# A tuned convolution block on Trainium2: one order of instructions on all engines, and the sampling's source blocks by DMA from a copy transposed once

## The chip, the cores and the metric

The kernel runs on one core of one Trainium2 chip. The core has five engines that run their own instruction streams side by side and wait for each other by semaphores: TensorE (PE, matrix products, with its weight loads listed as PEld), VectorE (DVE), ScalarE (ACT), GpSimd (POOL) and SyncE (SP, which here only issues DMAs). TensorE writes into PSUM, which is allocated in eight banks of 128 x 512 float32 values; the others mostly work in SBUF. The metric is the device time of one execution in microseconds. All data are float32.

## The reference

The input x has 32 images of 96 channels, 56 x 56 pixels. Two layers follow each other. The first is an inverted bottleneck: a 1x1 convolution to 576 channels, a 3x3 depthwise convolution, a squeeze-and-excite gate, a 1x1 convolution back to 96, and the input added. The second gates its input by a channel gate and a pixel gate (both computed from the image's spectrum), and convolves the gated image twice, once plainly and once with deformed sampling points:

```python
# first layer (bn: a per-channel scale and shift; fq: 8-bit rounding of the weights)
h = silu(bn1(conv1x1(x, fq(w1))))                    # 96 -> 576
h = silu(bn2(depthwise3x3(h, fq(w2))))
h = h * sigmoid(se_w2 @ silu(se_w1 @ mean(h) + se_b1) + se_b2)
x = x + bn3(conv1x1(h, fq(w3)))                      # 576 -> 96
# second layer
mag = abs(rfft2(x));      ca = channel_gate(mag)     # 96 values per image
sa = pixel_gate(mean_c(x), l2_c(x), resize(mean_c(mag)))   # 56 x 56 values
y = x * ca * sa
freq = resize(mean_c(abs(rfft2(y))))
aux = concat(y, coord, freq)
offset = conv3x3(aux, off_w)                         # 9 taps x (dx, dy) for each pixel
gate = sigmoid(conv1x1(relu(conv3x3(aux, dg1_w)), dg2_w))
y_base = conv3x3(y, base_w)
sampled = bilinear(y, pixel + offset)                # 9 samples per pixel and channel
y_def = einsum(sampled, def_w)
z = (1 - gate) * y_base + gate * y_def
out = relu(batchnorm(z) + x)                         # mean and variance over all 32 images
```

## The kernel before, in words

Work is laid out channels on partitions, pixels along the row. Images follow each other in a software pipeline; in the time of one image b the kernel samples and convolves b, computes the gates of b+1 and the hidden layer of b+2.

**The band loop** (`layers`, the loop over `bands`). An image is cut into 7 bands of 8 rows, and a band into two halves of 7 tiles (a tile is 4 columns wide and a half covers 28 columns; each tile has two 4-row groups). A half runs so:

- The bilinear sampling is a matrix product. For each tile the 8 x 8 pixels around it (64 source pixels, `NS`) are the contraction: `yt` holds these source blocks with pixels on partitions and channels along the row, 128 partitions for the two row groups; `wc` holds, for each source pixel, the sampling weight towards each tap of each output pixel. `sample_tiles` (L721) multiplies the two and ScalarE copies the result out of PSUM into `v` (L725). `pack` (L732) moves the last two taps beside the others, and `deform` (L740) applies `def_w` one half later.
- `yt` comes from `block_channels`: GpSimd copies the 8 x 8 blocks, with channels on partitions, from the padded gated image `yp` into `ybl` (L703, two copies for a half, one buffer), TensorE transposes seven blocks for each half into two banks (L707), ScalarE copies them into `yt` (L709).
- `wc` comes from `weights_load` and `weights`: four DMAs on SP spread the column weights and the row weights of a half over 128 partitions (`wc` L685, `wr` L686), and VectorE multiplies them (L692). `prepare` issues the loads, at the start of a half.
- After each tile of a half the loop calls `next(more)` and `pump()`. `more` is the generator `offsets` for the band two ahead: the joint 3x3 convolution of gate, offset and a third of the base (L605), the rest of the base convolution (L633), the offsets to DRAM (`od`, L655) and back (`ht`, L667), two ScalarE steps (L670, L671), and the finished hat functions to DRAM (`hd`, L674).

**The pump.** `pump` advances two generators: `first(b+2)` is `hidden`, whose depthwise taps are VectorE's multiply-adds (L261), with its expansion on TensorE (L168, evicted at L172) and its store `h2d` (L223); `second(b+1)` is `attend`: the projection from `h2d` (`hq` L305, L323, L329), the residual sum on GpSimd (L466), the spectrum (`dft_mag`: x loads L361, products L386 and L410, squares L413, sums L414, root L417), the gates, the spectrum of the gated image (L366 gates it on GpSimd), and the results `ca`, `sa`, `fq`. There are 17 pump steps in a band, 119 in an image. Each generator has a due time for its next step, a linear share of the image:

```python
streams[:] = [[second(b + 1), 0, n_second, slot + 3, slot + length - 8],
              [first(b + 2), 0, n_first, slot, slot + length]]
```

From band 5 (`turn`) the next image replaces this one in `yp`: `refill` loads rows of x1 (L584), the pixel gate `sab` (L586), and VectorE multiplies (L592).

**What sets the order of the work.** Every engine runs its own queue in order. Only SP's queue stands in the order of the text; the order on the other four is made by the framework's scheduler, which rearranges their instructions by its own costs:

```python
with tc.manual_schedule(engines={mybir.EngineType.SP}):
    layers(tc, a, dp, x1d, zd, stats, far)
```

PSUM is split into six banks that rotate (`mm`), one for the gates (`acc`) and one for the deformed convolution (`pd`). After the last image `normalise` reads z and x1 again, scales and writes the output.

## Time and profile before

| | |
|---|---|
| median of 3 runs | 9654.11 us (9645.51 to 9654.31) |
| profiled execution, its own time | 9648.5 us |
| its span, first to last instruction | 9646.7 us |
| mean granted TensorE clock | 0.923 |
| busy: PE, DVE, ACT, POOL | 8472.7, 7227.2, 5322.1, 2532.6 us |
| DMA | 1485.98 MB, mean 154 GB/s |

The page shows the busy time and share of each engine; the span in 40 slices, one digit each, busy share in tenths; the granted clock of TensorE in the same slices; then groups of instructions by line: destination and source, shapes, count, busy time, mean nanoseconds of one, the idle time of the engine just before them and what ended it. A row of waits names the waiting engine and line, what it waited for, the total in us, the number of times, and the longest. A row of windows gives, for a stretch, the busy time of PE, PEld, DVE, ACT and POOL (with the number of instructions), the granted clock, the share of the 16 DMA engines and the GB/s moved. The last 2.5% of the span are `normalise`, with the DMA engines full at 417 GB/s.

### The profile page before, as it was taken

To read this page: it belongs to the slowest core of one execution; us is meant where nothing else is said; L and a number is where in the kernel's file an instruction comes from. 1 tells how busy PE (TensorE), PEld (TensorE's weight loads), DVE (VectorE), ACT (ScalarE), POOL (GpSimd) and SP (SyncE) were. 2 spreads that over 40 slices of the span, in tenths; PEclk is the share of its full clock that TensorE was granted. 3 is DMA by queue.
4 is the path that set the end of the run, shared out by engine and by line. 5 is a ranking of instruction groups with operands and counts; after the bars stand their busy time and mean duration, and the time that the engine had idled before them with its cause. 6 is when DMAs were issued, how large, how long until landed. Compare 5 with 4: busy or idle time off the path is not lost. (4 is left out here: it accounts for less than half of the span.)

```text
span 9646.7 us, 129705 instructions
## 1 busy us (share of the span) xinstructions
PE 8472.7 (88%) x48374; PEld 5064.2 (52%) x48374; DVE 7227.2 (75%) x6948; ACT 5322.1 (55%) x10262; POOL 2532.6 (26%) x2642
## 2 busy tenths in 40 slices
PE   6889989998999999999899989999999999999870
PEld 3455555555555555555555555555555555555540
DVE  7688777778777787877777887777878777777323
ACT  2355555565555556555555655555555555565453
POOL 1123223222222322222232322233222323322210
PEclk9899999999999999999999999999999999999985
DMA  2355555555555555555555555555555555554449
GB/s 94 95 143 148 151 152 160 150 149 143 147 155 154 160 154 145 145 149 155 154 160 155 145 142 153 151 158 154 153 139 145 150 157 157 153 152 135 130 154 417
DMA packets 1069473, 1485.98 MB, mean 154 GB/s; under 512 B 590438, under 2 KB 840086, under 8 KB 1056550
## 3 DMA queue, kind: packets, MB, share of 16 engines
q1 hardware_dynamic: 858747, 985.20, 37.9%
q10 hardware_dynamic: 153803, 329.80, 9.2%
q0 software_dynamic: 56288, 162.60, 6.7%
q8 instruction: 388, 6.36, 0.3%
q14 instruction: 247, 2.02, 0.1%
HBM read 1064.29 MB, written 412.65 MB: 153 GB/s over the span
## 5 line engine op out<-in xcount | busy, mean ns | idle before, releaser
L261 DVE SCALAR_TENSOR_TENSOR acch<-hp,w,acch 128x1512 f32<-128x1512 f32 (+1 forms) x2250 | 4320.5, 1920 | 32.8
L605 PE MATMUL mm<-yp,c_jointW 104*128 104x448 f32 x4032 | 1649.0, 561 | 9.0 <-ACT yt L709 5.5
L740 PE MATMUL pd<-v,c_def 128*96 128x224 f32 (+1 forms) x6272 | 1414.8, 376 | 127.6 <-ACT v L732 104.1
L703 POOL COPY ybl<-yp 96x448 f32<-96x448 f32 x896 | 1014.7, 1159 | 1903.7 <-PE mm L707 1903.3
L721 PE MATMUL mm<-wc,yt 64*96 64x144 f32 x12544 | 1168.1, 308 | 153.5 <-DVE yb L638 76.8
L740 PEld LDWEIGHTS pd<-v,c_def 128*96 128x96 f32 (+1 forms) x6272 | 1051.8, 173 | 437.4 <-ACT v L732 142.5
L168 PE MATMUL mm<-xt,w 96*128 96x392 f32 (+3 forms) x2688 | 1136.3, 561 | 133.8 <-ACT yt L709 96.0
L605 PEld LDWEIGHTS mm<-yp,c_jointW 104*128 104x128 f32 x4032 | 783.6, 196 | 806.0 <-issue 762.6
L721 PEld LDWEIGHTS mm<-wc,yt 64*96 64x96 f32 x12544 | 884.2, 167 | 489.8 <-issue 188.0
L221 ACT ACTIVATE acch<-acch,sh,inv 128x1568 f32<-128x1568 f32 x288 | 487.5, 1693 | 1159.0 <-DVE acch L261 1143.9
L692 DVE TENSOR_TENSOR wc<-wc,wr 128x1008 f32<-128x1008 f32 x448 | 564.6, 1260 | 704.2 <-DMA wr<-hd 690.5
L725 ACT COPY v<-mm 96x288 f32<-96x288 f32 (+1 forms) x2688 | 1003.6, 442 | 117.7 <-PE mm L721 78.9
L172 ACT ACTIVATE hp<-mm,sh,inv 128x392 f32<-128x392 f32 (+2 forms) x1216 | 811.8, 672 | 326.9 <-PE mm L168 282.1
L633 PE MATMUL mm<-yp,c_base0W 96*64 96x448 f32 x4032 | 913.5, 550 | 0.0
L323 PE MATMUL mm<-hq,w3s 128*96 128x392 f32 x2048 | 788.2, 531 | 127.4 <-DMA hq<-h2d 125.9
L655 POOL DMA_DIRECT2D od<-at x224 | 186.3, 832 | 2275.1 <-DVE at L651 1451.9
L732 ACT COPY v<-v 32x448 f32<-32x448 f32 x1344 | 755.3, 562 | 30.3
L168 PEld LDWEIGHTS mm<-xt,w 96*128 96x128 f32 (+1 forms) x2688 | 389.9, 189 | 495.1 <-issue 264.8
L709 ACT COPY yt<-mm 128x384 f32<-128x384 f32 (+1 forms) x896 | 350.9, 441 | 491.5 <-PE mm L707 489.4
L323 PEld LDWEIGHTS mm<-hq,w3s 128*96 128x96 f32 x2048 | 336.3, 173 | 477.7 <-issue 382.5
L466 POOL TENSOR_TENSOR o<-o,xc 96x392 f32<-96x392 f32 x256 | 396.5, 1549 | 643.9 <-ACT o L333 642.3
L633 PEld LDWEIGHTS mm<-yp,c_base0W 96*64 96x64 f32 x4032 | 294.6, 134 | 515.5 <-issue 490.2
(194 smaller groups left out, 9023.7 us busy)
## 6 DMA issues: line engine op xcount, KB each, us to landing
h2d<-acch ACTq DMA_DIRECT2D x288, 784.0 KB
wc<-hd SPq DMA_DIRECT2D x896, 252.0 KB
wr<-hd SPq DMA_DIRECT2D x896, 252.0 KB
hq<-h2d SPq DMA_DIRECT2D x128, 980.0 KB
hq<-h2d SPq DMA_DIRECT2D x128, 784.0 KB
x<-x1d SPq DMA_DIRECT2D x768, 98.0 KB
ht<-od SPq DMA_DIRECT2D x224, 252.0 KB
hd<-ht ACTq DMA_DIRECT2D x224, 252.0 KB
```

What stands on the lines that cost most here:

```text
L168: nc.tensor.matmul(pt[p0 : p0 + w1.shape[1], : rows * W], w1, xts[hf][:, r0 * W : (r0 + rows) * W], start=True, stop=True)
L172: nc.scalar.activation(h1[lo:hi, row0 : row0 + rows, 1 : 1 + W], pt[lo:hi, : rows * W].rearrange("p (h w) -> p h w", h=rows), AF.Silu, bia ...
L261: nc.vector.scalar_tensor_tensor(acc[:, lo:hi], win, wk, acc[:, lo:hi], ALU.mult, ALU.add)
L323: nc.tensor.matmul(pts[half][:C, :EW], w3s[:, ch], hq, start=(i == 0), stop=False)
L605: nc.tensor.matmul(view, weights[:, k], yp[:channels, r0 : r0 + RB, dx + PD - 1 : dx + PD - 1 + W], start=(k == 0), stop=(k == NTAP - 1))
L633: nc.tensor.matmul(pb[k % 2 * BC : (k % 2 + 1) * BC, :BW].rearrange("p (h w) -> p h w", h=RB), w["base"][:, k], yp[:C, r0 : r0 + RB, dx + ...
L692: nc.vector.tensor_tensor(wc, wc, wr, ALU.mult)
L703: nc.gpsimd.tensor_copy(yb[:, :, s], blocks)
L721: nc.tensor.matmul(pt[k][:C, (t - lo) * KP : (t - lo + 1) * KP], yt[ps, t], s[ps, t * KP : (t + 1) * KP], start=True, stop=True)
L725: nc.scalar.copy(v[:C, :, lo:hi, k].rearrange("c k t p -> c t k p"), pt[k][:C, : (hi - lo) * KP].rearrange("c (t k p) -> c t k p", t=hi - ...
L732: nc.scalar.copy(v[C:, 1 + 2 * i : 3 + 2 * i], v[i * QC : (i + 1) * QC, KA:])
L740: nc.tensor.matmul(out.rearrange("c q (t x) -> c t q x", x=TS), p["w"]["def"][ks, k], v[ks, k].rearrange("c t s (r x) -> c t (s r) x", r=T ...
```

## The change

1. `manual_schedule()` names no engine: all five engines take their instructions in the order of the text, without the scheduler.
2. The text is rewritten for that. `attend`, `squeeze`, `dft_mag` and `offsets` are cut into smaller steps, with a `yield` between a product and what reads it; `hidden` yields after every tap, and expands the next image's first unit at the end of this one. `pump` takes exactly one step of `attend` in a slot, from slot 3 on. The two square roots of an image wait (`at_conv`) until the loop comes past a joint convolution.
3. The source blocks come from DRAM. When a row group of the gated image has been written to `yp` and multiplied, TensorE transposes it once (`turn_rows`, four products, one for each column phase), ScalarE copies it out, and GpSimd's queue stores it into `turned`, a copy laid out [column phase, row, column group, channel], one for each of two images. `block_load` reads a half's `yt` with four DMAs on SP. `block_channels` goes, and `yt` has three buffers where it had two. The order of the source pixels in a block is now columns first, so the two broadcasts of `wc` and `wr` are exchanged.
4. `prepare` is called after the weights of a half have been multiplied, for one half further ahead, and loads `yt` along with `wc` and `wr`. The first rows of the next image are asked for in band 4, not 5.

```diff
-        nc.sync.dma_start(wc[ps], src[2 * s].unsqueeze(0).to_broadcast([SB, SB, NTH * KP]))
-        nc.sync.dma_start(wr[ps], src[2 * s + 1].unsqueeze(1).to_broadcast([SB, SB, NTH * KP]))
+        nc.sync.dma_start(wc[ps], src[2 * s].unsqueeze(1).to_broadcast([SB, SB, NTH * KP]))
+        nc.sync.dma_start(wr[ps], src[2 * s + 1].unsqueeze(0).to_broadcast([SB, SB, NTH * KP]))
...
-def block_channels(nc, p, yp, j, h):
+def turn_rows(nc, p, yp, r0, r1):
+    n = (r1 - r0) * NTY
+    every = yp[:C, PD + r0 : PD + r1].rearrange("c h w -> c (h w)").rearrange("c (n x) -> c x n", x=TS)
+    pt = bank(p)
+    for x in range(TS):
+        nc.tensor.transpose(pt[:n, x * C : (x + 1) * C], every[:, x], p["w"]["ident"][:C, :C])
+    return pt
+
+def store_turned(nc, p, pt, yT, r0, r1):
+    n = (r1 - r0) * NTY
+    yq = p["yq"].tile([RB * NTY, TS, C], FP, name="yq")
+    nc.scalar.copy(yq[:n].rearrange("p x c -> p (x c)"), pt[:n, : TS * C])
+    nc.gpsimd.dma_start(yT[:, PD + r0 : PD + r1].rearrange("x h t c -> (h t) x c"), yq[:n])
+
+def block_load(nc, p, yT, j, h):
     yt = p["yt"].tile([2 * NS, NTH, C], FP, name="yt")
-    yb = p["ybl"].tile([C, NTH, 2, SB, SB], FP, name="ybl")
-    src = yp[:C, j * RB : j * RB + SB, h * NTH * TS : h * NTH * TS + SB]
     for s in range(2):
-        blocks = bass.AP(src.tensor, src.offset + s * TS * WY, [src.ap[0], [TS, NTH], [WY, SB], [1, SB]])
-        nc.gpsimd.tensor_copy(yb[:, :, s], blocks)
-    for lo, hi in ((0, 4), (4, NTH)):
-        pt = bank(p)
-        for t in range(lo, hi):
-            nc.tensor.transpose(pt[:, (t - lo) * C : (t - lo + 1) * C], yb[:, t].rearrange("c s r x -> c (s r x)"),
-                                p["w"]["ident"][:C, :C])
-        nc.scalar.copy(yt[:, lo:hi].rearrange("p t c -> p (t c)"), pt[:, : (hi - lo) * C])
+        for g in range(2):
+            r0, t0 = j * RB + s * TS, h * NTH + g
+            q0 = s * NS + g * TS * SB
+            nc.sync.dma_start(yt[q0 : q0 + TS * SB], yT[:, r0 : r0 + SB, t0 : t0 + NTH])
     return yt
...
         def start(b, length):
-            streams[:] = [[second(b + 1), 0, n_second, slot + 3, slot + length - 8],
-                          [first(b + 2), 0, n_first, slot, slot + length]]
+            streams[:] = [[second(b + 1), 0, slot + 3], [first(b + 2), 0, slot, length]]
...
+        def attended(b, args, r, r1):
+            attend_rows(nc, p, b, *args)
+            later.append((slot + 3, lambda: turn(b, r, r1)))
+
+        def turn(b, r, r1):
+            pt = turn_rows(nc, p, yp, r, r1)
+            later.append((slot + 1, lambda: store_turned(nc, p, pt, turned[b % 2], r, r1)))
...
             for h in range(2):
                 v = p["vp"].tile([128, NTAP, NTH, 2, TP], FP, name="v")
-                prepare(2 * n + h + READY + AHEAD)
                 s = ready.pop(0)
                 yt = yts.pop(0)
...
                         ready.extend(weights(nc, *ws) for ws in loads[:1])
                         del loads[:1]
-                        if h == 0:
-                            yts.append(block_channels(nc, p, yp, j, 1))
+                        prepare(2 * n + h + READY + AHEAD + 1)
+                        if b + 1 < B and j == TURN - 1 and h == 1:
+                            refill(b + 1, TURN * RB - PD)
...
-    with tc.manual_schedule(engines={mybir.EngineType.SP}):
+    with tc.manual_schedule():
         layers(tc, a, dp, x1d, zd, stats, far)
```

In `offsets` the distances change like this (the old form had seven steps between the `od` store and the `ht` load, and six from there to L670):

```diff
+    od = p["dp"].tile([NTX, 2, NOFF, TP], FP, name="od")
+    nc.gpsimd.dma_start(od.rearrange("t s o p -> o (t s) p"), at.rearrange("o t s p -> o (t s) p"))
     pb = bank(p)
...
     nc.vector.tensor_tensor(yb[:BC], yb[:BC], pb[BC:, :BW], ALU.add)
-    for _ in range(4):
-        yield
+    yield
+    nc.vector.tensor_reduce(top, at.rearrange("o t s p -> o (t s p)"), AX.X, ALU.max, apply_absolute_value=True)
+    yield from wait(2)
     ht = p["ht"].tile([SB * NTX, 4, KP], FP, name="ht")
...
     nc.sync.dma_start(ht.rearrange("q n k -> q (n k)"), src)
-    for _ in range(6):
-        yield
-    p["tc"].keep_in_program_order(nc.scalar.activation(ht, ht, AF.Abs, bias=w["blk"]))
+    yield from wait(4)
+    nc.scalar.activation(ht, ht, AF.Abs, bias=w["blk"])
```

## The prediction

> **What bounds the kernel now.** I read the page's parts 1 and 2 first, then TensorE's waits, the windows of one image, and last the DMA share of very short windows.
>
> ```profile
> span 9646.7 us, 129705 instructions
> PE 8472.7 (88%) x48374; PEld 5064.2 (52%) x48374; DVE 7227.2 (75%) x6948; ACT 5322.1 (55%) x10262; POOL 2532.6 (26%) x2642
> PE   6889989998999999999899989999999999999870
> PEclk9899999999999999999999999999999999999985
> 600.00:8880.00 8280.00, 7597.75 (x43811) 4542.08 (x43811) 6546.23 (x6028) 4771.26 (x9270) 2355.75 (x2400) 0.94 0.55 151
> ```
>
> TensorE (PE) is busy 7597.75 of 8280 us (92%) in the steady stretch, at a granted clock of 0.94; VectorE (DVE) has 79%, ScalarE (ACT) 58%. So TensorE bounds it, with 682 us idle and some clock missing. One image takes 276 us (the statistics of L1053 start at 798.2 first and 9360.7 last, 31 intervals).
>
> ```profile
> L707 PE MATMUL mm<-c_ident,ybl 96*128 96x96 f32 x3136 | 355.6, 250 | 85.7 <-ACT sq L413 80.3 <-POOL ybl L703 4.5 <-DVE sq L372 0.9
> L703 POOL COPY ybl<-yp 96x448 f32<-96x448 f32 x896 | 1014.7, 1159 | 1903.7 <-PE mm L707 1903.3
> L709 ACT COPY yt<-mm 128x384 f32<-128x384 f32 (+1 forms) x896 | 350.9, 441 | 491.5 <-PE mm L707 489.4 <-ACT acch L221 0.4
> PE mm L168 <- ACT yt L709: 96.0, 44, 5.2
> DVE wc L692 <- DMA wr<-hd: 690.5, 152, 18.3
> SPq L361 <- PE mm L386: 1272.9, 144, 52.9
> PE mm L323 <- DMA hq<-h2d: 125.9, 31, 9.4
> 4800.00:4810.00 10.00, 4.94 (x39) 3.49 (x31) 1.76 (x2) 0.76 (x3) 0.00 (x0) 0.96 0.56 166
> 4810.00:4820.00 10.00, 7.00 (x27) 4.30 (x28) 8.92 (x6) 9.86 (x19) 2.67 (x2) 0.50 0.00 0
> ```
>
> The first three rows are the block path that goes. The next shows it holding TensorE up. The two windows show the typical stall: VectorE sits 9.4 us in front of a weight product (L692) whose transfer is late, ScalarE's squares (L413) wait for VectorE, TensorE's transposes for a bank behind them; all engines fall idle, and TensorE then runs 10 us at clock 0.50. The SP row says that SP, kept in text order, stood up to 52.9 us before a load whose buffer TensorE frees later than the text has it, and everything after it in SP's queue, the weights too, stood with it.
>
> **The change part by part.** The sum is made against the profiled execution, 9648.5 us (span 9646.7), which is 5.6 below the median of 9654.11.
>
> *Block path on TensorE.* 3136 transposes go; four come for each row group written, and there are 255 groups (as many as the attend products of L592, x255), so 1020. A transpose costs 355.6/3136 = 0.113 us of TensorE's busy time: 2116 x 0.113 = **-240**, on the bounding engine. The new ones read a strided weight (every fourth column), which no row shows; with no price they cost as L707's, at twice it +116, at the range's end. Waits that the path itself ended on TensorE: 96.0 + 5.5 (L168 and L605 for L709) + 85.7 (L707's own idle) = **-187**.
>
> *Block path elsewhere.* ScalarE loses 641 copies of 0.39 us (-251), GpSimd 1014.7 us of copies; it gains 255 store issues, by the nearest row (od, L655: 504 pieces, 0.83 us) 212 us. Both lie beside TensorE: counted at nothing. GpSimd's queue no longer stands 1903 us before L703, so the gating products (L366) and the residual sums behind it start sooner. The store is issued behind sab, zd and od in that queue; it has whole bands before the first block load reads it, since the rows are filled from band 4 on and read for band 0 of the next image from band 6. If that lead were gone, the cost is its landing, 3.2 us as od, per image: 100 us.
>
> *Weights asked for earlier.* Before, the loads of wc and wr are issued at the start of a half band and multiplied three pump steps later: 3 x 276/119 = 7 us, and the transfer alone takes 8 us (below). After, they are issued just behind the previous product, a half band (276/14 = 19.7 us) ahead. VectorE's 690.5 us of waits mostly end. VectorE has slack; what counts is their echo on TensorE: L721 for yb 76.8, L430 for m_fe and m_fy 83.1, L386 for POOL x 34.3, L531 for cx 23.3, together 217; I take half, **-109** (bounds 0 and -217).
>
> *One order on all engines.* SP's long waits come from two orders that disagree. With one order a load behind a buffer is released when TensorE reaches the same place in the text. The rewritten steps put a consumer one step behind its producer. In return, each engine now waits in order for whatever the text names, which a scheduler might have filled. The trace of before cannot show this; bounds: -300 (half of the 682 us idle, less what is counted above) and +400 (a stall of 1.8 us in each of 224 bands, as ht's: the text between the od store and the ht load shrinks from seven steps to five, and from there to ScalarE's L670 from six to four; behind L670 on ScalarE stand the evictions that free TensorE's banks; its row is 79.2 us of waits now). I take 0.
>
> *Clock.* The stall shown costs about 6 us of clock per image (10 us at 0.50, some at 0.85): 32 x 6 = 192, of which I take half, **-95**.
>
> *New transfers.* Each half band gains four loads of 32 pieces of 2688 bytes, 344 KB; SP issues 1792 more DMAs at about 0.5 us (x has 0.45, wr 0.57): 2.1 us of SP's 19.7 per half, off the path but in front of every later load. What matters is which DMA engines carry them. Here is a stretch in which only wc and wr move:
>
> ```profile
> 4827.00:4829.00 2.00, 2.00 (x11) 1.00 0.51 123
> 4829.00:4831.00 2.00, 2.00 (x16) 1.00 0.52 127
> 4990.00:5000.00 10.00, 10.00 (x63) 1.00 0.95 250
> 5000.00:5010.00 10.00, 6.19 (x16) 0.86 0.90 263
> ```
>
> The columns at the end are clock, DMA share and GB/s. The share stands at 0.52: eight of 16 engines, 16 GB/s each, about 8 us for the 1.03 MB of a half. The Trainium skill ("DMA: Bandwidth & Descriptors", section "Why a DMA increments its semaphore by 16 and not by 1") says why: the number of engines is the largest up to 16 that divides the slowest dimension of both sides, on the SP queue the lowest-numbered ones. For wc that is 8, as the row shows. A block load has 32 partitions on one side and four column phases on the other: by the rule 4 engines, and always the same four, which carry wc and wr too. No run shows that yet. If the loads spread over 16 engines, a half needs 344/16/16 = 1.3 us per engine and this term is 0. By the rule it is 86/16 = 5.4 us on four engines, beside wc and wr's 8: 13 of 19.7 us. This stays inside the half in most of an image, but not while hq is loaded (the last two windows: 0.90 to 0.95 already, and TensorE waits): some 16 steps or 37 us, in which the four engines need hq 26 (4 x 1764 KB over 16 engines at 17 GB/s), weights 15, blocks 10 (1.9 halves each), others 4, so 55. The lead of a half takes most of the 18 us over; I take 5 us per image, **+150**, bounds 0 and 18 x 31 = +560.
>
> Sum: 9648.5 - 240 - 187 - 109 - 95 + 150 = 9167.5; on the median's scale 9173, so **9175 us**, 5% below.
>
> **The rivals.**
> *Four DMA engines become the bound (slower).* In the steady stretch the mean share 0.55 is 2430 engine-us per image. Less wc and wr (14 x 8 engines x 8 us = 896) and ht (7 x 16 = 112) it leaves 89 us per engine; the low eight carry 89 + 112 + 14 = 215 of 276 us. Block loads add 14 x 5.4 = 76, the stores about 10: 301 us per image, 25 more than now. If packets of different queues excluded each other, the end would be 9648 + 31 x 25 = 10420; the point from which it decides is a per-engine demand above the period that TensorE would need, some 262 us. Against it: short windows show shares above 1 (4839 to 4840: 1.21 at 360 GB/s), so the queues of one engine overlap; and SP's queue alone (q1, 37.9% of 16 x 276 = 1674; less 896 and 112, 42 per engine) comes to 42 + 112 + 14 + 76 = 244 us; the tail moves 417 GB/s, 26 per engine, so 16 is no ceiling. Chance 0.15.
> *In-order waits eat the gain.* TensorE loses the transposes but each band stalls for ht, hq or a bank as reckoned above, and the stalls bring back clock 0.50: +400 to +700 on 9175, 9575 to 9875. For: the shorter ht distances, SP's busier queue. Against: ScalarE has 42% free. Chance 0.14.
> *The stalls were nearly all of disagreeing orders.* Then idle falls from 8% to 4% and the clock rises to 0.98: 682/2 = 340 and 4% of 7598 = 300 beside the 240 of work, and no DMA price: 8770. For: the idle in the windows comes with late weights and banks. Against: hq's 125.9 stays. Chance 0.17.
> That the change does not do what it says is no rival here: the built program has the counts above.
>
> **How the numbers follow.** Forecast case 0.54 (own range 8900 to 9500), better case 0.17 (8550 to 8900), in-order case 0.14 (9500 to 9900, a third of it still below before), four engines 0.15 (9700 to 10500). This kernel's measurement can tell 0.2% from no change, about 19 us. Faster 0.54 + 0.17 + 0.05 = 0.76; same 0.02; slower 0.22. A range of 8700 to 9850 leaves out about a tenth on each side.
>
> **What would show it right or wrong.** Right: the rows of ybl and its copies gone, 1020 transposes near 0.11 us each; VectorE's wait for wr well under 300 us; no window near clock 0.50 in the squares stage; SP's wait on L386 far shorter at its longest; TensorE still the busiest at 92% or more. Block loads on four engines: a DMA share near 0.25 where only they move, and longer waits of L323 for hq. Wrong: TensorE's busy share under 88% with waits for yt, wr or hq on top (four engines); waits on ScalarE's ht or on banks spread over the bands (in-order case); a transpose that takes twice L707's time.

## The result, and the profile after

The changed kernel takes 10819.4 us (median of 4 runs, 10811.75 to 10832.39), against 9654.21 us for the kernel before beside it: a ratio of 1.1207, 95% interval 1.1187 to 1.1226. It is 12% slower where 5% faster was forecast.

The page of the changed kernel, parts 1 and 2:

```profile
span 10810.0 us, 126658 instructions
...
PE 8405.8 (78%) x46258; PEld 4991.7 (46%) x46258; DVE 7113.3 (66%) x6948; ACT 5080.6 (47%) x9623; POOL 1677.1 (16%) x2001
...
PE   5778877878887887887888788788778777878870
...
PEclk9788888888888888888888898888889888888885
...
L715 PE MATMUL mm<-c_ident,yp 96*120 96x96 f32 x1020 | 205.0, 350 | 753.0 <-DVE yp L620 750.1
```

No engine of this row is busier than before: every busy time fell. TensorE's share fell from 88 to 78%, and what grew is the time in which it does nothing: 10810.0 - 8405.8 = 2404 us, against 9646.7 - 8472.7 = 1174. TensorE has 2116 products fewer (x48374 to x46258). The transposes' own row gives back 355.6 - 205.0 = 151 us, yet TensorE's busy time fell by only 67. The clock has a part in that: the mean granted clock fell from 0.923 to 0.858, and products that run at a lowered clock take longer. Sorted by the clock granted while each ran, a joint convolution's product (L633) takes 544 ns on average at clock 1.0 and 965 at 0.50 in this trace, and 1681 us of TensorE's busy time lie at a lowered clock, where it was 1046 before. An image takes 310.6 us (the statistics of L1097 start at 888.1 first and 10516.1 last, 31 intervals) instead of 276.

The waits of the changed kernel (engine, line, what it waited for: total us, times, longest):

```profile
PE mm L715 <- DVE yp L620: 750.1, 135, 16.5
...
PE mm L352 <- DMA hq<-h2d: 328.8, 73, 9.3
PE mm L408 <- DMA x<-x1d: 294.6, 35, 11.5
...
ACT yq L723 <- DMA turned<-yq: 663.3, 139, 14.5
...
DVE wc L705 <- DMA wr<-hd: 45.3, 10, 9.6
...
SPq L682 <- DMA od<-at: 1609.5, 125, 54.7
SPq L698 <- DMA hd<-ht: 1215.1, 101, 20.3
SPq L381 <- PE mm L408: 876.6, 69, 38.5
```

Line numbers moved: L715 are the new transposes, L352 is L323 of before, L408 is L386, L705 is L692, L682 is L667, L698 is L685, L381 is L361. Three rows answer to rows of the prediction. VectorE's wait for `wr` fell from 690.5 to 45.3 us. TensorE's wait for `hq` rose from 125.9 to 328.8, and that for the image loads `x` from 17.9 to 294.6. SP's wait for TensorE fell from 1272.9 to 876.6, but its waits for `od` and `hd` rose (777.1 to 1609.5, 702.6 to 1215.1): it still stands, only elsewhere. The rows of before that the prediction does not show:

```profile
PE mm L386 <- DMA x<-x1d: 17.9, 3, 11.9
...
SPq L667 <- DMA od<-at: 777.1, 83, 15.1
...
SPq L685 <- DMA hd<-ht: 702.6, 42, 24.3
```

At the top of TensorE's waits in the changed kernel is one that did not exist: the new transposes stand before rows that VectorE has not yet multiplied.

This happens once in every image, at the turn of the band loop. Here is one turn. Windows of the changed kernel (length, busy of PE, PEld, DVE, ACT, POOL, then clock, DMA share, GB/s), and below them the timeline of the same stretch (start, us, engine, line):

```profile
5190.00:5200.00 10.00, 10.00 (x64) 7.09 (x64) 7.64 (x10) 6.48 (x14) 1.52 (x3) 1.00 0.59 157
5200.00:5210.00 10.00, 2.72 (x22) 1.51 (x20) 9.86 (x7) 5.27 (x10) 0.00 (x0) 0.87 0.69 211
5210.00:5220.00 10.00, 1.76 (x8) 1.21 (x8) 4.39 (x4) 2.84 (x5) 1.02 (x2) 0.50 0.65 153
5220.00:5230.00 10.00, 1.76 (x8) 1.22 (x8) 3.47 (x4) 0.00 (x0) 1.83 (x3) 0.50 0.79 194
```

```profile
5204.90 10.32 SPq L612 DMA_DIRECT2D yp<-x1d  x5
...
5215.98 1.90 PE L715 MATMUL mm<-c_ident,yp 96*120 96x96 f32 x8 [12.52 <-DVE yp L620]
...
5216.13 0.51 POOL L614 DMA_DIRECT2D sab<-sad  x1 [24.61 <-DVE yp L620]
...
5221.44 0.88 PE L715 MATMUL mm<-c_ident,yp 96*120 96x96 f32 x4 [3.55 <-DVE yp L620]
...
5225.55 0.88 PE L715 MATMUL mm<-c_ident,yp 96*120 96x96 f32 x4 [3.23 <-DVE yp L620]
...
5230.31 0.85 PE L715 MATMUL mm<-c_ident,yp 96*90 96x96 f32 x4 [3.88 <-DVE yp L620]
```

TensorE is full until 5200, then works 6.2 us in 30, the last 20 of them at clock 0.50. SP takes 10.32 us to ask for five row groups of the next image; GpSimd stood 24.61 us before the third `sab`, which needs the buffer of an earlier product; VectorE multiplies a row group when both are there; and TensorE, whose queue is in text order, stands at each group's transposes (12.52, 3.55, 3.23, 3.88 us). Everything that the text has after them waits too: the joint convolution of the next image's first band, which reads the same rows, and the sampling of the running image.

The block loads do run on four engines. Two windows of the changed kernel, the first with `wc` and `wr` alone on the move, the second with `yt` alone:

```profile
5070.00:5072.00 2.00, 2.00 (x7) 0.82 (x5) 1.97 (x2) 1.90 (x2) 0.00 (x0) 1.00 0.52 127
...
5077.00:5078.00 1.00, 1.00 (x6) 0.49 (x5) 1.00 (x4) 0.00 (x0) 0.49 (x1) 1.00 0.25 99
```

A share of 0.25 is four of 16, as the rule of the Trainium skill that the prediction weighed ("DMA: Bandwidth & Descriptors", section "Why a DMA increments its semaphore by 16 and not by 1") has it; which four they are, no view shows. But each of the four carries 99/4 = 25 GB/s, where `wc` and `wr` get 127/8 = 16 from each of theirs. A half's 344 KB take 344/99 = 3.5 us, not the 5.4 us of the prediction.

### The profile page after: what moved, and what is told of

Same layout as the page of the kernel before. It is cut to its first block, busy times and chain, and to the rows that moved or that the text cites. A ratio compares the mean times of both kernels' runs of the same rounds, so it can differ in the third digit from the quotient of the medians.

```text
span 10810.0 us, 126658 instructions
## 1 busy us (share of the span) xinstructions
PE 8405.8 (78%) x46258; PEld 4991.7 (46%) x46258; DVE 7113.3 (66%) x6948; ACT 5080.6 (47%) x9623; POOL 1677.1 (16%) x2001
## 5 line engine op out<-in xcount | busy, mean ns | idle before, releaser
L287 DVE SCALAR_TENSOR_TENSOR acch<-hp,w,acch 128x1512 f32<-128x1512 f32 (+1 forms) x2250 | 4178.0, 1857 | 38.0
L633 PE MATMUL mm<-yp,c_jointW 104*128 104x448 f32 x4032 | 1681.5, 572 | 67.2 <-ACT hp L191 64.6
L765 PEld LDWEIGHTS pd<-v,c_def 128*96 128x96 f32 (+1 forms) x6272 | 1106.1, 180 | 450.4 <-issue 131.1
L662 DVE COPY at<-mm 18x224 f32<-18x224 f32 x448 | 154.4, 380 | 1757.2 <-ACT yb L658 1755.2
L633 PEld LDWEIGHTS mm<-yp,c_jointW 104*128 104x128 f32 x4032 | 795.5, 200 | 862.3 <-issue 764.5
L352 PE MATMUL mm<-hq,w3s 128*96 128x392 f32 x2048 | 860.5, 573 | 378.6 <-DMA hq<-h2d 328.8
L187 PE MATMUL mm<-xt,w 96*128 96x392 f32 (+3 forms) x2688 | 1059.3, 546 | 69.7 <-DMA xt<-in_x 45.5
L746 PE MATMUL mm<-wc,yt 64*96 64x144 f32 x12544 | 1038.4, 303 | 34.0 <-issue 13.6
L746 PEld LDWEIGHTS mm<-wc,yt 64*96 64x96 f32 x12544 | 834.4, 167 | 430.7 <-issue 329.7
L715 PE MATMUL mm<-c_ident,yp 96*120 96x96 f32 x1020 | 205.0, 350 | 753.0 <-DVE yp L620 750.1
L352 PEld LDWEIGHTS mm<-hq,w3s 128*96 128x96 f32 x2048 | 368.6, 189 | 801.7 <-issue 747.3
L408 PE MATMUL mm<-c_FU,x 112*128 112x116 f32 x3072 | 436.2, 296 | 300.7 <-DMA x<-x1d 294.6
L705 DVE TENSOR_TENSOR wc<-wc,wr 128x1008 f32<-128x1008 f32 x448 | 564.2, 1259 | 45.3 <-DMA wr<-hd 45.3
L723 ACT COPY yq<-mm 120x384 f32<-120x384 f32 x255 | 121.2, 475 | 982.5 <-DMA turned<-yq 663.3
```

What stands on the lines that cost most here:

```text
L187: nc.tensor.matmul(pt[p0 : p0 + w1.shape[1], : rows * W], w1, xts[hf][:, r0 * W : (r0 + rows) * W], start=True, stop=True)
L287: nc.vector.scalar_tensor_tensor(acc[:, lo:hi], win, wk, acc[:, lo:hi], ALU.mult, ALU.add)
L352: nc.tensor.matmul(pts[half][:C, :EW], w3s[:, ch], hq, start=(i == 0), stop=False)
L408: nc.tensor.matmul(pt[:, i * 4 * V : (i + 1) * 4 * V], x2s[g][:, 2 * i : 2 * i + 2, :].rearrange("h c w -> h (c w)"), w["FU"], start=True, ...
L633: nc.tensor.matmul(view, weights[:, k], yp[:channels, r0 : r0 + RB, dx + PD - 1 : dx + PD - 1 + W], start=(k == 0), stop=(k == NTAP - 1))
L705: nc.vector.tensor_tensor(wc, wc, wr, ALU.mult)
```

## The experiments

All ratios are to the kernel before, timed beside each; one per cent is 97 us. The letters are used below. First the parts of the change, and what the order has to do with it.

**a. The scheduler again.** The changed kernel, with the four compute engines ordered by the scheduler as before.

```diff
-    with tc.manual_schedule():
+    with tc.manual_schedule(engines={mybir.EngineType.SP}):
```

> The changed kernel with one line undone: only SP keeps the text order, the scheduler orders the other four engines again; the blocks still come by DMA. Theory 1 (the rewritten order stalls TensorE behind the refill at the image's turn, 750 us of waits of L715 for L620) and theory 3 (in-order waits everywhere) expect 9200 to 9700 us, L715's wait for L620 under 200 us. Theory 2 (the block loads on four DMA engines are the price) expects over 10500 us, since the same loads stay.

10883.54 us, ratio 1.1258 (1.1239 to 1.1277): no better. TensorE's wait at L715 fell to 405.3 us, and others took its place; VectorE's wait for `wr` is back, at 963.4 us. So the loss is not cured by giving the order back.

**f. The order alone.** The kernel before, its text unchanged, with all engines in text order (and without the call that keeps L670 in place, which text order implies).

```diff
-    p["tc"].keep_in_program_order(nc.scalar.activation(ht, ht, AF.Abs, bias=w["blk"]))
+    nc.scalar.activation(ht, ht, AF.Abs, bias=w["blk"])
...
-    with tc.manual_schedule(engines={mybir.EngineType.SP}):
+    with tc.manual_schedule():
```

> The kernel before with its old text, but all engines in the order of the text. If order alone is the loss, 10300 us or more, with TensorE's waits on ScalarE and VectorE spread over the bands; if the order matters little (a_scheduler moved only 64 us), 9550 to 9900 us.

10553.1 us, ratio 1.0927 (1.0905 to 1.095). The old text is not fit to be run in its own order.

**g. Text and order, without the new block path.** The changed kernel with `block_channels` of before in place of the turned copy.

```diff
-                b, j = bands[n]
-                yts.append(block_load(nc, p, turned[b % 2], j, m))
...
+        yts = [block_channels(nc, p, yp, 0, 0)]
...
+                        if h == 1 and n + 1 < len(bands):
+                            yts.append(block_channels(nc, p, yp, bands[n + 1][1], 0))
```

> The changed kernel with the old block path (GpSimd's copies, 14 transposes a band, from yp), its wc and wr broadcasts as before and no turning; the rewritten text, one order on all engines and the later prepare stay. Theory A expects 10200 us or more. Theory B expects 9700 us or less, with no wait of TensorE behind the attend product at the turn and hq's wait near 130 us.

10148.21 us, ratio 1.0505 (1.0481 to 1.0529). The rewriting wins back nearly half of what the order costs in f, and still stands 5% above the kernel before. Waits of TensorE in g:

```profile
PE mm L633 <- DMA yp<-fqd: 169.1, 20, 10.2
PE mm L720 <- POOL ybl L716: 168.2, 125, 4.5
PE mm L408 <- DMA x<-x1d: 149.7, 40, 7.1
...
PE mm L633 <- DVE yp L620: 94.5, 12, 8.8
...
PE acc L539 <- ACT s L536: 68.6, 32, 2.5
```

The first and the fourth are the refill of `yp` at the turn: without the new transposes TensorE stands at the joint convolution instead. The second is the old block path itself: in text order its transposes stand 168.2 us before GpSimd's copies, where under the scheduler they stood 4.5. The last is one of a dozen of its kind, each link of the gates' chain met once an image a microsecond or two early.

**e. The block path alone.** The kernel before with source blocks by DMA (point 3 of the change), the old text, the scheduler, and two `yt` buffers (so the third buffer of the change is in neither e nor g).

```diff
-                            yts.append(block_channels(nc, p, yp, bands[n + 1][1], 0))
...
+                b, j = bands[n]
+                yts.append(block_load(nc, p, turned[b % 2], j, m))
```

> The kernel before, with the block path by DMA and nothing else: its old text, its scheduler, prepare at the start of a half; yt keeps two buffers. Theory A (the new text is the loss, the DMA path is worth its 240 us of TensorE) expects 9200 to 9650 us. Theory B (the DMA path itself costs: loads on four engines and the turning at the image's turn; c_no_loads and d_no_turn gave back 521 and 437 us) expects 9900 to 10400 us.

9984.53 us, ratio 1.0342 (1.0318 to 1.0365). Each half of the change (e is point 3, g the points 1, 2 and 4) loses by itself: 1.0342 x 1.0505 = 1.0864, and both together give 1.1207, so some 3% comes only from the two in one kernel.

**l. The new text under the scheduler** (g with SP alone in text order, as in a).

> Experiment g (the new text in its own order on all engines, old block path, 10148.2) with the order on the four compute engines made by the scheduler again; SP stays in text order. If the new text alone is what costs (its one step of attend per slot, its cut into small steps, SP's new order), the scheduler recovers little: 10050 to 10250. If the order on the engines is what costs, it returns to the kernel before: 9600 to 9750.

10425.65 us, ratio 1.0796 (1.0764 to 1.0828), worse than g. The new text is fitted to its own order: the scheduler undoes that and does not restore the kernel before.

**Inside the changed kernel: c, d, b, h.**

**c. No block loads.** The sampling reads one tile of zeros; turning and storing stay.

```diff
+        fixed = p["cp"].tile([2 * NS, NTH, C], FP, name="fixed")
+        nc.gpsimd.memset(fixed, 0.0)
...
-                yts.append(block_load(nc, p, turned[b % 2], j, m))
+                yts.append(fixed)
```

> The changed kernel without the 1792 block loads: the sampling reads one fixed tile of zeros; turning and storing stay. Theory 2 expects 9900 us or less, with the waits of L352 for hq (329 us) and L408 for x (295 us) back near 130 and 20. Theory 1 expects 10450 to 10800 us, and L715's wait for L620 unchanged near 750 us.

10298.16 us, ratio 1.0663 (1.064 to 1.0686): 521 us less than the changed kernel. Waits of TensorE in c:

```profile
PE mm L715 <- DVE yp L620: 648.4, 138, 11.1
PE mm L408 <- DMA x<-x1d: 216.2, 59, 6.4
...
PE mm L352 <- DMA hq<-h2d: 70.5, 67, 4.8
```

The wait for `hq` falls from 328.8 to 70.5 and that for `x` from 294.6 to 216.2. The wait at the turn stays.

**d. No turning.** Only images 0 and 1 are transposed and stored.

```diff
         def turn(b, r, r1):
+            if b >= 2:
+                return
```

> The changed kernel in which only the first two images are turned and stored; all others read those copies. It leaves out some 950 transposes, 240 copies and 240 stores. Theory 1 in its narrow form (the transposes themselves block TensorE's queue) expects 9900 to 10200 us; in its wide form (the refill is late, and the joint convolution of the next image waits for the same rows) L633 takes over the wait and the time stays over 10400 us. Theory 2 expects 10600 to 10750 us, for the stores and the transposes' own 100 us alone.

10382.32 us, ratio 1.0744 (1.0726 to 1.0762), 437 us less. One wait of TensorE in d:

```profile
PE mm L633 <- DMA yp<-fqd: 449.5, 30, 18.6
```

With the transposes of the turn gone, over half of their 750 us reappears at the next reader of the refilled rows, L633; the row that it waits for, `fqd`, is the last load of the refill in SP's queue. So the hole at the turn is the late refill, more than the transposes that first run into it.

**b and h. The refill earlier.** In b it is asked for half a band earlier; in h besides its groups are asked for two steps apart.

```diff
-                        if b + 1 < B and j == TURN - 1 and h == 1:
+                        if b + 1 < B and j == TURN - 1 and h == 0:
```

> The changed kernel, with the refill of the next image's first 38 rows asked for in the first half of band 4, not the second (one digit), so some 8 pump steps earlier. Theory 1 expects L715's wait for L620 to fall from 750 to under 300 us and the time to 10000 to 10400 us. Theories 2 and 3 expect a time within 150 us of 10819.

> The changed kernel, with the refill of 38 rows begun half a band earlier and its five groups asked for one after another, two pump steps apart (loads, five steps later the product, then the turning), so that GpSimd's queue no longer stands before the third sab load. If the queue behind the refill is what costs at the turn, 10200 to 10450 us, with L715's wait for L620 under 150 us and SP's wait for od under 700 us; if it is the transposes and loads as such, within 100 us of b_refill_early's 10699.

10699.43 us (1.1073, 1.1054 to 1.1092) and 10723.55 us (1.1101, 1.1077 to 1.1126). In b TensorE's wait at L715 fell from 750.1 to 265.6 us, but the time only by 120; spreading the loads adds nothing.

**Engines or bytes: i and j.**

**i. The same bytes on 16 engines.** In the changed kernel each load reads 32 consecutive rows of one phase, so that the slowest dimension of both sides is 32. The pixels are then other ones.

```diff
-            nc.sync.dma_start(yt[q0 : q0 + TS * SB], yT[:, r0 : r0 + SB, t0 : t0 + NTH])
+            r0 = min(r0, HY - TS * SB)
+            nc.sync.dma_start(yt[q0 : q0 + TS * SB], yT[s * 2 + g, r0 : r0 + TS * SB, t0 : t0 + NTH])
```

> The changed kernel, but each of the four block loads of a half reads 32 consecutive rows of one column phase of the copy instead of 8 rows of each of the four phases: the same bytes, pieces of 2688 bytes and number of DMAs, with 32 as outermost count instead of 4. The pixels that the sampling then sees are the wrong ones; nothing else changes. Theory A (the loads cost because they sit on four engines, behind the weights' loads there): a load's transfer shares out over 16 engines, the image's x and hq loads no longer wait behind engines 0 to 3, and most of the 521 us that taking the loads away gave comes back: 10300 to 10500. Theory B (they cost because of their bytes and of their place in SP's queue, 0.6 us of issue each and their wait for a free yt buffer): 10700 to 10820.

10598.01 us, ratio 1.0982 (1.0951 to 1.1013): between the two theories. Of the 521 us that the loads cost, 221 go when they are spread. No stretch of i has `yt` alone on the move, so the spread itself is not seen as a share. Waits of TensorE in i:

```profile
PE mm L408 <- DMA x<-x1d: 243.8, 35, 8.9
...
PE mm L352 <- DMA hq<-h2d: 196.9, 73, 6.2
```

**j. One load per row group in the old text.** Experiment e with a copy in which 64 source pixels stand at one stride.

```diff
-            nc.sync.dma_start(yt[q0 : q0 + TS * SB], yT[:, r0 : r0 + SB, t0 : t0 + NTH])
+        src = bass.AP(yT.tensor, yT.offset + (r0 * NROW + t0 * SB) * C, [[NTY * C, SB * SB], [SB * C, NTH], [1, C]])
+        nc.sync.dma_start(yt[s * NS : (s + 1) * NS], src)
...
-    nc.gpsimd.dma_start(yT[:, PD + r0 : PD + r1].rearrange("x h t c -> (h t) x c"), yq[:n])
+    for g in range(2):
+        dst = bass.AP(yT.tensor, yT.offset + ((PD + r0) * NROW + g * (TS * NTY - SB)) * C, [[SB * C, n], [NTY * C, TS], [1, C]])
+        nc.gpsimd.dma_start(dst, yq[:n])
```

> The kernel before with only the source blocks by DMA (experiment e), but the copy laid out so that the 64 source pixels of a row group stand at one uniform stride (a column of a block every 15 units of 96 channels, a row every 120, a tile every 8): one DMA per row group, two for a half instead of four, with 64 as the outermost count; the price is pieces of 384 bytes instead of 2688, and a second store for each row group that is turned. The order of pixels in a block is rows first again, so wc and wr are spread as before. The computation is the reference's. Experiment e stood at 9984.5. Theory A (four engines): the loads fall off the path, and the 240 us of removed transposes begin to show: 9600 to 9800. Theory B (bytes and issues, not engines): SP has half the issues, the engines see pieces a seventh as long: 9900 to 10100. Theory C (the turning at the image's turn is what costs in e): no change, 9950 to 10050.

9993.54 us, ratio 1.0345 (1.0314 to 1.0377), the same as e. Half the issues and more engines brought nothing in the sum, though the two waits fell, as the table below shows: TensorE's waits for ScalarE's copies out (`yq`) grew from 157 to 254 us, since ScalarE's wait for the stores of `yq` grew from 314.1 to 491.8: there are two for a group instead of one.

**What the block path costs and could bring, in the old text: o, p, s, r.** o is e with the cut of d, p is e with the cut of c. r is the kernel before with nothing in place of its block path; p and r sample from zeros (in r that product takes 302 ns on average, 308 before). s is e with the loads on GpSimd's queue; its edit:

```diff
-            nc.sync.dma_start(yt[q0 : q0 + TS * SB], yT[:, r0 : r0 + SB, t0 : t0 + NTH])
+            nc.gpsimd.dma_start(yt[q0 : q0 + TS * SB], yT[:, r0 : r0 + SB, t0 : t0 + NTH])
```

and the edit of r (`fixed` is the tile of zeros of c):

```diff
-                yt = yts.pop(0)
+                yt = fixed
...
-                            yts.append(block_channels(nc, p, yp, bands[n + 1][1], 0))
...
-                            yts.append(block_channels(nc, p, yp, j, 1))
```

> Experiment e (old text, source blocks by DMA, 9984.5), with the turning (transposes, copy out, store) of images 0 and 1 alone; later images sample from the copies of those two, so the sampled values are of the wrong image from image 2 on. Theory A (the turning costs: its work of 28 transposes at 0.2 us and 7 copies an image, 180 us in all, and the waits for the refilled rows): 9650 to 9780. Theory B (the loads cost, the turning hides): 9880 to 9980.

> Experiment e (9984.5) without the block loads: the sampling reads one tile of zeros, the turning and its stores stay. Theory A (the turning costs): 9850 to 9980. Theory B (the loads cost, by their bytes and SP's issues, since 16 engines instead of four brought nothing in experiment j): 9550 to 9750. In the rewritten text the same cut gave 521 us.

> Experiment e (9984.5), with the four block loads of a half on GpSimd's queue instead of SP's[...]. If the loads cost by standing in SP's queue (0.6 us of issue each, and 651 us in which SP stands at a block load until the sampling frees its yt buffer, with the x and hq loads behind): near experiment p without loads, 9690 to 9780. If they cost by their bytes: 9930 to 10000. If GpSimd's queue holds them up behind its own waits (744 us for the refill's sab): 10000 to 10300.

> The kernel before without its block path: no GpSimd copies into ybl, no transposes (3136 of them, 355.6 us of TensorE in the profile before), no copies into yt (395 us of ScalarE); the sampling reads one tile of zeros. Nothing is put in their place. If the time follows TensorE's work and the waits that the block path ends (85.7 us before the transposes, 96.0 before L168): 9100 to 9250. If TensorE's work that goes leaves TensorE waiting for the next chain (squares, gates, image loads), as experiment p suggests: 9400 to 9560. If it changes nothing: 9630 to 9670.

| kernel | us | ratio, interval | TensorE waits for `hq` | for `x` | for `yq` copies |
|---|---|---|---|---|---|
| before | 9654 | 1 | 125.9 | 17.9 | |
| r, no block path | 9410.48 | 0.9725 (0.9703 to 0.9748) | 137.2 | 20.1 | |
| p, turning, no loads | 9688.07 | 1.0027 (1.0016 to 1.0038) | 132.5 | 17.3 | 208 |
| o, loads, no turning | 9854.52 | 1.0202 (1.0176 to 1.0228) | 287.9 | 231.8 | 2 |
| e, both | 9984.53 | 1.0342 (1.0318 to 1.0365) | 287.1 | 174.4 | 157 |
| j, both, 64 rows a load | 9993.54 | 1.0345 (1.0314 to 1.0377) | 214.3 | 45.6 | 254 |
| s, both, loads by GpSimd | 10290.32 | 1.0638 (1.0605 to 1.0671) | 267.5 | 15.6 | 294 |

(The waits for `yq` are summed over all of TensorE's lines that stand behind a bank which the copy at L711 or L712 must empty.)

The two waits behave differently. That for `hq` stays at 267.5 when the loads leave SP's queue and is back at 132.5 only without them; in the new text, spreading them alone took it from 328.8 to 196.9 (i), and leaving them out to 70.5 (c). So the loads reach `hq`, the largest transfer, at least in part through the DMA engines. The wait for `x` is 174 to 232 with four loads of a half on SP, and 16 to 20 with none there (p, s, r). Yet in j it is 45.6 with two loads on SP, so the place behind SP is not the whole of it, and whether the fewer issues or the more engines help in j was not separated. In the new text the wait for `x` is 216.2 even without the loads (c).

How SP comes to stand shows in e and, for as long, in j; what takes its place shows in s:

```profile
SPq L722 <- DMA hd<-ht: 753.5, 93, 10.8
SPq L722 <- PE mm L734: 650.6, 91, 14.8
```

```profile
SPq L724 <- PE mm L736: 701.1, 97, 14.6
```

```profile
POOL yt L722 <- PE mm L734: 1627.0, 311, 21.6
...
L722 POOL DMA_DIRECT2D yt<-turned x1792 | 1090.7, 614 | 2063.6 <-PE mm L734 1627.0 <-PE acc L478 219.3 <-PE acc L285 89.2
```

In the old text, with two `yt` buffers, a block load waits until the sampling (L734, in j L736) frees its buffer, and whichever queue it is on waits with it: 651 us on SP, 1627 on GpSimd, which also pays 1091 us of issue and carries the residual sums and the gating of the images. But standing there is not what makes `x` late: in j SP stands as long as in e, and `x` waits a quarter as long. In the changed kernel, with three buffers, no wait of SP at its block loads (L734 there) is for the sampling; the longest are for DMAs:

```profile
SPq L734 <- DMA hq<-h2d: 200.7, 93, 5.1
...
SPq L734 <- DMA h2d<-acch: 155.2, 44, 6.9
```

Nor is s a clean test of the queue alone: GpSimd's queue cuts the loads otherwise. Its page has 143360 packets more than e's on queue q0 and 64512 fewer on q1, 80 for a load where it was 36.

What turning and loading cost depends on which of them is there already: turning costs 3.0% without the loads (p against r) and 1.4% with them (e against o), the loads 3.2% beside the turning (e against p) and 4.8% without it (o against r).

**Weights asked for early: k and n.** k is the kernel before with the one step of the change that the prediction priced at -109; n undoes it in g.

```diff
-                prepare(2 * n + h + READY + AHEAD)
...
                         del loads[:1]
+                        prepare(2 * n + h + READY + AHEAD + 1)
```

> The kernel before with one thing from the change: the weights' loads of a half are asked for behind the previous half's product, for one half further ahead, instead of at the half's start. The step of the prediction that counted this at -109 us: 9500 to 9600. If VectorE's wait for wr (690 us in the kernel before) is no cause of TensorE's waits, because the scheduler put other work there: 9630 to 9680. If the loads, asked for in the middle of a half, only move in front of the image's x and hq loads in SP's queue: 9680 to 9800.

> Experiment g (new text in its own order on all engines, old block path, 10148.2), with the weights' loads of a half asked for at the half's start again, as in the kernel before, instead of behind the previous half's product for one half further. If the early asking costs here what it cost in the old text (205 us in experiment k): 9920 to 9980. If it is the scheduler's planning around it that cost there, and queues in text order profit from early loads: 10140 to 10400, VectorE's wait for wr growing to some 700.

k: 9859.25 us, ratio 1.0199 (1.0171 to 1.0227). n: 10062.46 us, ratio 1.0417 (1.0392 to 1.0442), 0.9% below g. Early asking costs in both texts. VectorE's wait for `wr` is 372.7 us in n and 10.8 in g, and n is the faster: ending that wait by asking earlier gained nothing. Waits in k:

```profile
PE mm L721 <- DVE yb L638: 192.2, 90, 6.6
PE mm L386 <- POOL x L366: 177.4, 57, 7.4
...
PE mm L323 <- DMA hq<-h2d: 17.7, 9, 7.0
...
DVE wc L692 <- DMA wr<-hd: 743.6, 222, 20.0
...
SPq L685 <- DMA hd<-ht: 1575.5, 130, 26.6
```

VectorE waits for `wr` no less (743.6 against 690.5): the weights can't be read before ScalarE has written the hat functions to DRAM, and SP now stands at their load for that (1575.5 against 702.6 us). My third guess, that `hq` and `x` would be late behind it, is refuted (17.7 against 125.9 for `hq`, 16.4 against 17.9 for the loads of `x`). What grew on TensorE is the waits for `yb`, behind VectorE's late product (76.8 to 192.2), and for GpSimd's gating of `x` (34.3 to 177.4). Yet its idle time, span less busy, rose by only 53 us, to 1227; its busy time rose by 158 for the same products, at a clock of 0.905 instead of 0.923. Sorted by the clock, 341 us more of it lie at a lowered clock and 183 less at full clock. Counted in windows of 10 us from 1000 to 9200, 12% of them stand below clock 0.8 before and 18% in k (28% in the changed kernel, from 1000 to 10200).

**q. attend at an even pace.** g with the 81 steps of `attend` spread over the image as before, in place of one in every slot.

```diff
-            streams[:] = [[second(b + 1), 0, slot + 3], [first(b + 2), 0, slot, length]]
+            streams[:] = [[second(b + 1), 0, slot + 3, length - 11, n_second], [first(b + 2), 0, slot, length]]
...
-                due = slot - st[2] if len(st) == 3 else n_first * (slot - st[2]) / st[3]
+                due = (st[4] if len(st) == 5 else n_first) * min(1.0, (slot - st[2]) / st[3])
```

> Experiment g (10148.2), with attend's 81 steps spread linearly over the image's 108 slots, as in the kernel before, instead of one in every slot until it is done. If the quick start is what costs (TensorE waits on the gates' chain of small products, square roots and copies, one link per slot, and the last slots of an image without attend): 9850 to 10050. If one step per slot is as good as any pace: 10100 to 10200. If the gates then come too late for the refill at the turn: 10250 to 10500.

11660.66 us, ratio 1.2073 (1.2045 to 1.2102). The quick start is not what costs; it is what saves the new text. In q:

```profile
PE acc L594 <- DVE m_fy L590: 617.6, 32, 21.4
```

Once an image TensorE stands 19 us at the end of the second spectrum (`m_fy`, from which the map `fq` is made). Of the three guesses only the third, gates that come late, points this way, and it was too small by over 1100 us. This row is 618 of the 1500 us by which q is slower than g; the rest was not traced.

## Why the prediction was wrong, point by point

The measured 10819 lies above every case that the prediction named. The two largest failures are the order with the text rewritten for it, counted at nothing (g: +488 us), and the block path on its new way: its loads at +150 (c: 521), and its turning at nothing beyond the transposes (p against r: 290). The waits that were to be gained (-187, -109, -95) gave nothing: they ended, and others took their place. The parts were measured in different kernels and do not add up to the whole.

- **Transposes, -240: a mis-sized term.** The count was right (1020), the price was not: the new ones take 205.0/1020 = 0.201 us in the changed kernel, against 0.113 for the old, so they cost 205 us, not 115. A dearer price was named, put at the range's end and left out of the forecast. More than half of the rise goes with the clock: 768 of the 1020 ran at a clock of about 0.50, as in the turn shown, right behind TensorE's waits (of L707's it was 52 of 3136). At clock 1.0 one of 120 columns takes 284 ns against 247 for one of L707, at 0.50 it takes 374.
- **Waits that the block path ended, -187: failed.** r takes the whole path away and gains 2.75%, some 265 us, with 355.6 us of transposes gone. TensorE's idle time there is 9419.8 - 8239.0 = 1181 us, as before (1174). The waits named did end; others came in their place (L386 for the gated `x` 34.3 to 97.2, L430 for `m_fy` 40.0 to 113.4). I had not said what is late next. I had also misread the row of L707: 80.3 of its 85.7 us are a wait for a bank that the squares (L413) hold, which is not the block path's. In r 55.6 us of waits for these squares stand before other products. The rows of r:

```profile
PE acc L430 <- DVE m_fy L427: 113.4, 32, 11.6
...
PE mm L386 <- POOL x L366: 97.2, 48, 3.6
...
PE mm L721 <- ACT sq L413: 42.1, 20, 4.3
```

- **"Block path elsewhere", at nothing: failed.** p against r is the price of turning without the loads, 3.0% or 290 us: as much as the whole old path cost. Only 115 us of that were in the forecast, as transposes. In the two profiles 194 of 281 us are busy time of TensorE (151 the transposes) and 88 idle. In p 208 us of waits are for banks that ScalarE empties late, while the single `yq` waits for its store (379.7 us in p; 663.3 after). The store had lead over its reader, as I said; it had none over the next copy into its source. What a second `yq` would give was not tried.
- **Weights asked for earlier, -109: the wrong sign.** k: +2.0%. The wait of VectorE did fall in the changed kernel, to 45.3 us, but SP's for `hd` rose. n shows that in the new text, too, late asking is the better, though VectorE then waits 372.7 us: that wait had no echo worth counting.
- **One order on all engines, 0 within -300 and +400: at the upper bound or past it.** With the new text it is +5.1% (g), or +4.2%, some 400 us, without the early asking (n); with the old text +9.3% (f). ht, on which I had put the upper bound, is no part of it: ScalarE's L684 waits 47.6 us for it in all in the changed kernel. It is the refill at the turn, `x`, the old block path's transposes before GpSimd's copies (in g), and a dozen small waits in the gates' chain. g does not separate order from text, as l is worse than g.
- **Clock, -95: the wrong sign.** It fell as the idle time rose, 0.923 to 0.858.
- **New transfers, +150 within 0 and +560: the largest mis-sized term.** The loads cost 521 us in the changed kernel (c) and some 300 in the old text (e against p). I had the four engines right, and sized them by bytes over 16 GB/s. They were faster than that, and spreading them gave back only 221 of the 521. The other 300 are open: what I had waved through as "off the path but in front of every later load" is 1792 issues of about 0.63 us and the waits shown above, and no run took the issues away and left the bytes.
- **What held.** The wait for `wr` under 300 us; four engines, share 0.25; longer waits for `hq`; SP's longest wait at the image load shorter (52.9 to 38.5), though not far shorter. Of the signs that it was wrong, TensorE's share under 88% came; `hq` came second among TensorE's waits and not on top; a transpose took 1.8 times L707's time, not twice; waits for ht did not come.

Of the rivals, the in-order waits had the right mechanism and named the wrong waits; the four engines had a share, but a load on four engines is not the bound: spread (i), the kernel is still 9.8% slower.

Four things stay open. How the 3% that neither half shows alone comes about was not tried by itself; b and d point at the turn, where refill, transposes and stores meet. Why i and j differ in what spreading brings was not separated from j's smaller pieces and second store. By what way the loads cost the 300 us that spreading leaves is not shown. And no version here beats the kernel before while computing the same.

## What to carry to other kernels

Before replacing a block of work, run the kernel with the block simply left out: here that was 2.75%, and any replacement had to cost less than that on every queue. A load that must wait for a buffer or for a DRAM write makes everything behind it in its queue wait, so asking earlier (k), or from another queue (s), moved the wait and did not end it. A long wait that is ended is no gain by itself: VectorE's for the weights went, and the kernel was slower. Price a stall that goes by what is late next, and put the clock on the side of the stalls that come.

## What the runs showed of the hardware

- A transpose that reads every fourth column as its weight loads more slowly, and that is not the clock: sorted by the clock granted meanwhile, a load of 120 such columns takes 204 ns on average at clock 1.0 and 211 at 0.50 (the changed kernel), where a contiguous one of 128 columns takes 140 at clock 1.0 (before).
- A DMA engine's rate depended on the transfer: 25 GB/s for the block loads, 16 for the spread weights, by the two windows shown. What sets it was not tried.
- TensorE's clock cost more than its idle time in k: idle grew by 53 us, and busy time by 158 for the same products, more of which ran at a lowered clock.
